# A filter, Mamba and FFN pipeline on one core: two convolution taps in one matmul, and the scan's products moved in TensorE's order

## The chip, the cores and the metric

The kernel runs on one core of one Trainium2 chip. A time is the device time of one execution in microseconds (us). The core has five engines that work at once and meet only through semaphores: TensorE (PE in the profile), VectorE (DVE), ScalarE (ACT), GpSimd (POOL) and SyncE (SP), whose queue issues the DMA transfers. Each engine takes its own instructions strictly in the order in which the program lists them.

## The reference

The input is 8 images of 64 channels and 128 x 128 pixels. Each goes through two layers.

Layer 0 is a filter with weights that depend on the pixel: a 3x3 convolution to 32 channels, a leaky ReLU, a 1x1 convolution to 9 values, and a softmax over them. With those weights `w_lp` the output is `x + sum over k of shifted_k(x) * (delta_k - w_lp_k)`. As `delta` picks the pixel itself, this is twice the pixel less the weighted mean of its nine neighbours.

Layer 1 takes that as `input` and does, cut to what matters:

```python
x_norm = ln4d(input, ...)                 # layer norm over the 64 channels
seq = layernorm(pixels as a sequence of 16384)
for i in range(2):
    seq = bimamba_block(seq, ...)         # forward and backward selective scan, 128 channels x 16 states
x4 = conv2d(rmsnorm(seq), resconv_w, pad=1)              # 3x3, 64 -> 64
x_mamba = x4 + res
dw = conv2d(conv2d(x_norm, dw1_w), dw2_w, groups=64, pad=1)   # 1x1, then depthwise 3x3
x = input + dw * x_mamba
g1, g2 = split(depthwise 3x3 of conv2d(ln4d(x), ffn_in_w))    # 64 -> 340
return x + conv2d(gelu(g1) * g2, ffn_out_w)
```

## The kernel before, in words

Four kinds of work are laid beside each other. The **scan** (class `Chunk`) is the main one: for each image, two layers by two directions by 16 chunks of 1024 pixels, 512 chunks in all. A chunk has U = 16 steps; a step is one scan instruction over 128 (channel, state) rows by 1024 pixels. An image has therefore 1024 steps, and the run 8192. Beside the scan of image b run three background jobs, each in 16 tiles of eight image rows (two halves of four rows stand on the two halves of the partitions):

- **Front** (layer 0 and the norms) of image b + 1, from step 569 of the image on, one tile each 24 steps;
- **Mix** (the two 3x3 convolutions, the product with `dw`, a norm) of image b, around the change to the next image, one tile each 13 steps;
- **FFN** of image b, beside steps 180 to 560 of the next image, one tile each 24 steps.

The front of image 0 runs ahead of the first scan, and partly beside it. The FFN of image 7 runs alone at the end, while its mix stands beside the end of its own scan.

Order is written out by hand. Each piece of work is put down with `at(time, phase, function)`. A step has the phases FEED, SCAN, MID, PROD, DECAY and REST, in this order. At the end the pieces are taken by (step, phase), and within one such place in the order in which they were put down; chunks put theirs down before front, mix and FFN do. Every engine's instruction list follows from that, and so does SP's queue of transfers.

One step of the scan works like this. `drive` (L1048) lets POOL multiply `bu` from `dup` and `bp` for two steps at a time, into three buffers. `decay` (L1053) lets ACT write exp(dt * A) to `w`, in one of two PSUM buffers. `scan` (L1063) is DVE's. `product` (L1092) multiplies by C, on DVE or, for some steps, on POOL. `collect` (L1103) sums over states in TensorE, into the single bank `y`. So that these have their inputs, each chunk needs main products in TensorE two chunks ahead: `conv` (L922, tile xp), `gate` (L938, zp), `step` (L967, dp) and `bc` (L984, bcp), and behind the second direction `project` (L1142, op), means (ms) and spread (rb). All of these share one PSUM bank, "mm": each product waits until ACT (or DVE) has read the one before. They are put in the phase FEED, and their evictions by ACT in DECAY of the same step or the next (L1177 on).

Background uses two further banks, "acc" and "bg". In the front, `hidden` (L450) is the first 3x3 convolution, nine matmuls of one tap each over a window `xa` with the two halves' weights as diagonal blocks; `weight` (L505) spreads the nine softmax weights over channels, `weighted` (L515) multiplies with the window `xb` on DVE, and `gather` (L519) sums the nine products in TensorE, onto a first matmul with `ident2`, twice the identity, that puts in the doubled pixel. In the mix, `conv` (L653) does the depthwise and the full 3x3 convolution in the same way, nine matmuls each of 128 x 128. The FFN's `conv` (L740) already takes two taps a matmul: the window is loaded twice, the second copy shifted by one pixel, on the two halves of the partitions. `rest_times` (L818) is DVE's product of the gelu's last 42 channels.

Tiles of 512 pixels in SBUF come from one ring, `tmp` (L402, 14 buffers), windows from another, `win` (L405, 2 buffers).

Of the kernel before, what the change touches and what calls it, by code (L numbers as in the profile page):

```python
# [15 lines left out]
P = 128  # L16
C = 64
# [38 lines left out]
def kernel(ctx: ExitStack, tc: tile.TileContext, a: dict, out: bass.AP):  # L56
# [15 lines left out]
    def const(shape, name, dt=F32):  # L72
        return wp.tile(shape, dt, tag=name, name=name)
# [47 lines left out]
    nc.vector.memset(half_mean[C:P, 1:2], 1.0 / C)  # L121
    ident2 = const([P, P], "ident2")
    nc.vector.tensor_tensor(ident2, ident, ident, ALU.add)

    sel_k = const([54, 9, 2, C], "sel_k", BF16)
    for h in range(2):
        k18 = [
            identb[0:54, 18 * i + 9 * h : 18 * i + 9 * h + 9]
            .rearrange("k (m o) -> k m o", o=1).to_broadcast([54, 9, C])
            for i in range(3)  # L130
        ]
        nc.vector.tensor_tensor(sel_k[:, :, h, :], k18[0], k18[1], ALU.add)
        nc.vector.tensor_tensor(sel_k[:, :, h, :], sel_k[:, :, h, :], k18[2], ALU.add)
    nc.vector.tensor_scalar(sel_k, sel_k, -1.0, None, ALU.mult)


# [28 lines left out]

    FRONT_W, MIX_W, FFN_W = 9 * 64 + P, 18 * P, 18 * P + 2 * C + P + 2 * 9
    w_dram = [dram([P, n], f"w{i}") for i, n in enumerate((FRONT_W, MIX_W, FFN_W))]

    def front_weights(t):
        return t[:, 0 : 9 * 64].rearrange("p (k m) -> p k m", m=64), t[:, 9 * 64 : FRONT_W]  # L170

    def mix_weights(t):
        v = t[:, 0:MIX_W].rearrange("p (i k m) -> p i k m", i=2, m=P)
        return v[:, 0], v[:, 1]

# [5 lines left out]
    with tc.tile_pool(name="wspill", bufs=1) as fp, tc.tile_pool(name="wprep", bufs=2) as pp, \  # L181
            tc.tile_pool(name="wps", bufs=4, space=PSUM) as pps:
        wt = [fp.tile([P, n], F32, tag=f"w{i}", name=f"w{i}") for i, n in enumerate((FRONT_W, MIX_W, FFN_W))]
        w1, dw1 = front_weights(wt[0])
        dw2, wres = mix_weights(wt[1])
        wpair, wlast, wout_a, wout_b, win_b, wtap_b = ffn_weights(wt[2])

# [18 lines left out]
        def diagonal(col, n):  # L206
            d = pp.tile([P, P], F32, tag="diag", name="diag")
            nc.vector.tensor_scalar(d[0:n, 0:n], ident[0:n, 0:n], col, None, ALU.mult)
            return d[0:n, 0:n]

        for t in wt:
            nc.gpsimd.memset(t, 0.0)
# [14 lines left out]
        for k in range(9):  # L227
            to_blocks(w1[:, k, :], turned(w1t[:, k, :], ident[0:32, 0:32], P, 32), C, 32)
            to_blocks(wres[:, k, :], turned(resv[:, k, :], ident[0:C, 0:C], P, C), C, C)
            nc.vector.tensor_scalar(dw2[:, k, :], ident, dw2n[:, k : k + 1], None, ALU.mult)  # L230
        w2n = pp.tile([9, 32], F32, tag="w2n", name="w2n")
# [153 lines left out]
    def tmp(name):  # L385
        return wk.tile([P, N], F32, tag="tmp", name=name, bufs=14)

    def window(img, name):

        return inp.tile([P, ROWS + 2, PW], F32, tag="win", name=name)  # L390

# [7 lines left out]
    def tap(win, k):  # L399
        i, j = divmod(k, 3)  # L400
        return win[:, i : i + ROWS, j : j + W]
# [38 lines left out]
    class Front:  # L440
# [4 lines left out]

        def load_x(self, name):
            setattr(self, name, window(x_img, name))
            load_window(getattr(self, name), x_img, self.c)

        def hidden(self, i):  # L450
            w1, _ = front_weights(Bg.weights)
            if i == 0:
                self.hp = acc_tile("hp")
            for k in range(3 * i, 3 * i + 3):
                nc.tensor.matmul(self.hp[0:64, :], w1[:, k, :], tap(self.xa, k), start=(k == 0), stop=(k == 8))

# [44 lines left out]
        def turned(self):  # L501
            self.wt = wk.tile([54, N], BF16, tag="wt", name="wt", bufs=2)
            nc.scalar.copy(self.wt, self.tp.rearrange("p r w -> p (r w)"))

# [14 lines left out]
        def gather(self, k):  # L519
            if k == 0:  # L520
                self.acc = acc_tile("acc")
                nc.tensor.matmul(self.acc, ident2, tap(self.xb, 4), start=True, stop=False)
            nc.tensor.matmul(self.acc, ident, self.t.pop(k), start=False, stop=(k == 8))  # L523

# [23 lines left out]
        def pointwise(self):  # L548
            _, dw1 = front_weights(Bg.weights)
            self.dp = acc_tile("dwp")  # L550
            nc.tensor.matmul(self.dp, dw1, self.xn, start=True, stop=True)
# [29 lines left out]
        def plan(self, a):  # L581
            n1, n2, n3 = self.n1, self.n2, self.n3
            b = a - FRONT_STEP
            self.alone = a + FRONT_STEP < -2
            at(b - 5, REST, self.load_x, "xa")
            for i in range(3):
# [12 lines left out]
            at(b + 32, DECAY, self.turned)  # L599
            at(a + 6, REST, self.load_x, "xb")  # L600
            for k in range(9):
# [46 lines left out]
    class Mix(Front):  # L648
        def load_conv(self, img, name):
            setattr(self, name, window(img, name))  # L650
            load_window(getattr(self, name), img, self.c)

        def conv(self, which, win, i):  # L653
            w = mix_weights(Bg.weights)[which]
            if i == 0:
                self.cv = acc_tile("cv")
            for k in range(3 * i, 3 * i + 3):
                nc.tensor.matmul(  # L658
                    self.cv, w[:, k, :], tap(getattr(self, win), k), start=(k == 0), stop=(k == 8 and which == 0)
                )  # L660

# [27 lines left out]
        def plan(self, a):  # L689
            n1 = self.n1  # L690
            at(a - 5, REST, self.load_conv, dw_img[self.p], "dww")
            at(a - 4, REST, self.load_conv, xm_img, "xmw")
            at(a - 1, REST, self.load_h)
            for i in range(3):
                at(a + i, REST, self.conv, 0, "dww", i)
                at(a + 3 + i, REST, self.conv, 1, "xmw", i)
            at(a + 3, DECAY, self.branch_out)
            at(a + 2, REST, self.load_x1)
            at(a + 5, REST, self.add_h)
            at(a + 8, DECAY, self.times)  # L700
            at(a + 8, REST, self.plus)
            at(a + 10, REST, self.store_x2)
            at(a + 10, REST, self.centered, bg_tile, "x1")
            at(a + 11, DECAY, self.centered_out)
            at(a + 12, REST, lambda: n1.means(bg_tile, self.sq))
            at(a + 13, DECAY, n1.means_out)
            at(a + 13, REST, n1.root)
            at(a + 16, REST, n1.spread, bg_tile)
            at(a + 17, DECAY, self.scaled, n1)
            at(a + 17, DECAY, self.norm)  # L710
            at(a + 17, REST, self.store_rows, xn_img, "hc")
# [7 lines left out]
    class Ffn:  # L719
# [6 lines left out]
        def load(self, h):  # L726
            if not self.alone:
                self.win[h] = window(xn_img, "fw")
            else:
                if h == 0:  # L730
                    self.fw = wk.tile([P, 2, T], F32, tag="bu", name="fw", bufs=3)
                self.win[h] = self.fw[:, h, 0 : (ROWS + 2) * PW].rearrange("p (r w) -> p r w", w=PW)
            for i in range(2):
                lo = PW * first_row(self.c, h) + i
                nc.sync.dma_start(
                    self.win[h][C * i : C * i + C].rearrange("p r w -> p (r w)"),
                    xn_img[:, lo : lo + (ROWS + 2) * PW],
                )

# [113 lines left out]
        def plan(self, a):  # L853
# [19 lines left out]
            at(a + gelus, REST, self.gelus)  # L873
            at(a + gelus + 1, DECAY, self.rest_times)
            at(a + out - 5, REST, self.load_x2)
# [18 lines left out]
    class Chunk:  # L894
# [97 lines left out]
        def bc_out(self):  # L992
            self.bcs = wk.tile([64, N], F32, tag="bc", name="bc", bufs=1)
            nc.scalar.copy(self.bcs, self.bcp[0:64, :])

# [181 lines left out]
        def plan(self):  # L1177
            b = self.t0 - 2 * U
            at(b + 3, REST, self.load_hn)
            for h in range(2):  # L1180
                at(b + 7 + h, FEED, self.conv, h)
                at(b + 7 + h, DECAY, self.conv_out, h)
                if self.second:
                    at(b + 9 + h, FEED, self.gate, h)
                    at(b + 9 + h, DECAY, self.gate_out, h)
                at(b + 14 + h, FEED, self.step, h)
                at(b + 14 + h, DECAY, self.step_out, h)
# [4 lines left out]
            b = self.t0  # L1192
            at(b - 16, FEED, self.bc)
            at(b - 16, DECAY, self.bc_out)
# [34 lines left out]
            at(b + 2, REST, self.load_h)  # L1229
            at(b + 5, FEED, self.project)  # L1230
            at(b + 6, DECAY, self.residual)
            at(b + 6, DECAY, self.square)
            if self.l == 0:
                at(b + 7, REST, self.store_h)
            at(b + 12, FEED, lambda: n.means(mm_tile, self.sq))
            at(b + 13, DECAY, n.means_out)
            at(b + 14, REST, n.root)
            at(b + 17, FEED, n.spread, mm_tile)
            at(b + 18, DECAY, self.normed)
# [52 lines left out]
```

## Time and profile before

| what | value |
|---|---|
| median of 3 runs | 29687.24 us (29686.83 to 29689.91) |
| the profiled execution | 29750.91 us, its span 29749.1 us |
| first scan starts, last scan ends | at 581 us and 29290 us of the span |
| busy: DVE, POOL, PE, ACT | 92%, 93%, 81%, 62% of the span |
| mean granted TensorE clock | 0.88 of full speed |
| DMA traffic | 6617.94 MB, 222 GB/s |

A row of groups in the profile gives the line, the engine, the operation, the tiles (out<-in), the shape and the count; then the busy time of the group, the mean time of one, and the engine's idle time before them with what ended it. A row of waits gives engine, tile and line of what waited, what it waited for, the sum in us, how often, and the longest. In a stretch of the timeline, the idle time before an instruction stands in brackets.

### The profile page before, as it was taken

The page shows a single profiled execution, that of the slowest core. Times are in us where ns is not written, and L with a number is a line of the kernel's source. Part 1 is how long each engine was busy: PE and PEld are TensorE (multiplying, and loading weights), DVE is VectorE, ACT ScalarE, POOL GpSimd, SP SyncE. Part 2 cuts the span into 40 slices and gives each one's busy share as a digit, 9 for nine tenths or more (in the row PEclk, how much of TensorE's full clock was granted, in tenths as well). Part 3 has the DMA queues.
Part 4 walks back from the last instruction along what each step waited for, and adds up shares of the span by engine and source line. Part 5 has one row for each costly group of instructions (what it writes and reads, how often), then busy time and mean ns, then how long its engine had stood idle before and what let it go on. Part 6 is the DMA issues. An engine that isn't in the chain of part 4 may idle for free. (4 is left out here: it accounts for less than half of the span.)

```text
span 29749.1 us, 307276 instructions
## 1 busy us (share of the span) xinstructions
PE 24131.5 (81%) x95804; PEld 8066.2 (27%) x95804; DVE 27302.9 (92%) x17562; ACT 18550.1 (62%) x28366; POOL 27655.0 (93%) x8732
## 2 busy tenths in 40 slices
PE   7766888878888788887888788887888878888578
PEld 3211332223322233222332223222232222322123
DVE  3999999999999999999999999999999999999996
ACT  2666666666666666666666666666666666666663
POOL 2999999999999999999999999999999999999993
PEclk8777888988889888988889888998898988989789
DMA  4676677767777677776777767777676766777674
GB/s 99 219 246 218 218 233 233 238 212 222 237 232 235 211 227 236 236 231 211 231 233 237 227 213 233 234 237 222 217 233 229 242 219 220 234 231 240 212 238 124
DMA packets 2530818, 6617.94 MB, mean 222 GB/s; under 512 B 418982, under 2 KB 723382, under 8 KB 2526870
## 3 DMA queue, kind: packets, MB, share of 16 engines
q1 hardware_dynamic: 2529174, 6598.27, 69.4%
q8 instruction: 757, 12.40, 0.2%
q14 instruction: 887, 7.27, 0.1%
HBM read 5364.00 MB, written 1266.18 MB: 223 GB/s over the span
## 5 line engine op out<-in xcount | busy, mean ns | idle before, releaser
L1050 POOL TENSOR_TENSOR bu<-dup,bp 128x2048 f32<-128x2048 f32 x4096 | 18567.4, 4536 | 568.0 <-DVE w L1078 413.9
L1058 ACT ACTIVATE w<-dtp,a_neg 128x1024 f32<-128x1024 f32 x8192 | 9162.5, 1118 | 514.1 <-DVE hs L1076 318.6
L1100 DVE TENSOR_TENSOR hs<-w,cp 128x1024 f32<-128x1024 f32 x5360 | 6564.4, 1225 | 322.3 <-DMA cp<-bc_dram 90.2
L1097 POOL TENSOR_TENSOR hs<-hs,cp 128x1024 f32<-128x1024 f32 x2832 | 6677.2, 2358 | 180.4 <-ACT state L1090 116.2
L1076 DVE TENSOR_TENSOR_SCAN w<-w,state,bu 128x1024 f32<-128x1024 f32 x2677 | 6281.0, 2346 | 349.9 <-ACT w L1058 349.1
L1078 DVE TENSOR_TENSOR_SCAN w<-w,state,bu 128x1024 f32<-128x1024 f32 x2683 | 6290.8, 2345 | 312.5 <-ACT w L1058 311.9
L1116 PE MATMUL y<-hs,sel_y 128*32 128x512 f32 x32768 | 5185.5, 702 | 30.3 <-POOL hs L1097 30.0
L1090 ACT COPY state<-w 128x1 f32<-128x1 f32 x5360 | 836.7, 156 | 5064.1 <-DVE hs L1100 5028.9
L1076 DVE TENSOR_TENSOR_SCAN hs<-w,state,bu 128x1024 f32<-128x1024 f32 x1419 | 3321.0, 2340 | 55.4 <-PE y L1116 28.2
L1078 DVE TENSOR_TENSOR_SCAN hs<-w,state,bu 128x1024 f32<-128x1024 f32 x1413 | 3307.3, 2341 | 54.6 <-ACT w L1058 37.6
L1109 PE MATMUL y<-xc,dskip 128*64 128x512 f32 x4096 | 1635.9, 867 | 2009.1 <-ACT yv L1133 1334.8
L928 PE MATMUL xp<-hn,wx 128*128 128x512 f32 x4096 | 2262.7, 680 | 447.8 <-ACT xc L934 344.2
L760 PE MATMUL fp<-fw,bgw 128*128 128x512 f32 (+1 forms) x5760 | 2276.1, 642 | 66.1 <-ACT ga L807 64.7
L1116 PEld LDWEIGHTS y<-hs,sel_y 128*32 128x32 f32 x32768 | 739.0, 117 | 3492.7 <-issue 2462.8
L1090 ACT COPY state<-hs 128x1 f32<-128x1 f32 x2832 | 540.6, 191 | 1827.8 <-DVE hs L1078 929.3
L421 POOL TENSOR_TENSOR r<-r,neg_half 128x8 f32<-128x8 f32 x768 | 1261.8, 1643 | 373.9 <-ACT r L418 312.3
L934 ACT ACTIVATE xc<-xp,cbias 128x512 f32<-128x512 f32 x1024 | 696.5, 680 | 1351.3 <-PE xp L928 1351.1
L969 PE MATMUL dp<-xc,wdt 128*128 128x512 f32 x2048 | 1214.9, 677 | 362.2 <-ACT dt L976 282.0
L1058 ACT ACT_TABLE_LOAD x1134 | 1454.9, 1283 | 20.1
L766 PE MATMUL fp<-fw,bgw 64*128 64x512 f32 (+1 forms) x5760 | 1415.6, 610 | 0.0
L1006 POOL TENSOR_TENSOR dt<-dt,xc 128x1024 f32<-128x1024 f32 x512 | 1211.0, 2365 | 207.9 <-DMA dt_dram<-dt 186.4
L523 PE MATMUL acc<-t,ident 128*128 128x512 f32 x2304 | 1369.5, 679 | 4.3 <-DVE t L517 4.3
(198 smaller groups left out, 27172.3 us busy)
## 6 DMA issues: line engine op xcount, KB each, us to landing
bp<-bc_dram SPq DMA_DIRECT2D x4096, 256.0 KB, 4.1
dup<-du_dram SPq DMA_DIRECT2D x4096, 256.0 KB, 5.0
dtp<-dt_dram SPq DMA_DIRECT2D x4096, 256.0 KB, 5.0
cp<-bc_dram SPq DMA_DIRECT2D x4096, 256.0 KB, 5.0
hn<-hn_dram SPq DMA_DIRECT2D x1024, 256.5 KB, 5.0
dt_dram<-dt SPq DMA_DIRECT2D x512, 512.0 KB, 3.4
du_dram<-dt SPq DMA_DIRECT2D x512, 512.0 KB, 2.6
yf_dram<-yv SPq DMA_DIRECT2D x512, 256.0 KB, 4.5
```

The costliest lines, as they stand in the source:

```text
L760: nc.tensor.matmul(o, wpair[:, i, g, m], self.win[h][:, i : i + ROWS, 0:W], start=(i == 0), stop=False)
L766: nc.tensor.matmul(o, wlast[rows, i, g, m], self.win[h][rows, i : i + ROWS, lo : W + lo], start=False, stop=(i == 2),)
L928: nc.tensor.matmul(self.xp[h], wx[:, self.l, self.d, i, :], self.hn2[:, s.start + 2 * i : s.stop + 2 * i], start=(i == 0), stop=(i == 1),)
L1050: nc.gpsimd.tensor_tensor(bu, self.dup[self.pairs[k][1]], self.over_pair("bp", k), ALU.mult)
L1058: nc.scalar.activation(w, self.dtp[gp][:, i, :], AF.Exp, scale=a_neg[:, self.l, self.d, g, j : j + 1])
L1076: nc.vector.tensor_tensor_scan(to, w, bu, s0, ALU.mult, ALU.add)
L1078: nc.vector.tensor_tensor_scan(to[:, ::-1], w[:, ::-1], bu[:, ::-1], s0, ALU.mult, ALU.add)
L1090: nc.scalar.copy(self.column(u), h[:, T - 1 : T] if self.d == 0 else h[:, 0:1])
L1097: nc.gpsimd.tensor_tensor(hs, hs, c, ALU.mult)
L1100: nc.vector.tensor_tensor(hs, w, c, ALU.mult)
L1109: nc.tensor.matmul(self.y[C * h : C * h + C, :], dskip[:, self.l, self.d, C * gp : C * gp + C], self.xc[:, s], start=True, stop=False,)
L1116: nc.tensor.matmul(self.y[lo : lo + 32, :], sel_y, hs[:, i, s], start=False, stop=(k % 4 == 3))
```

## The change

Five things are changed together.

1. The hidden convolution of the front and both convolutions of the mix use `two_halves`, which does for them what the FFN's convolution did: a window of each half is loaded twice, shifted by one pixel; the taps j = 0 and 1 of a row are one matmul of 128 rows, and the tap j = 2 is a matmul over the 64 rows of the half. For nine taps there are 12 matmuls, each for one half's columns, in place of 9 for both.
2. `ident2` and its matmul go. The bias row of ones is added to the transposed softmax weights `wt` (row 64, so 65 rows in place of 54), and the selector `sel_k` has 2 there for tap 4: the weight of the middle tap comes out as 2 less its softmax weight.
3. The products conv, gate, step, bc, project, means and spread of a chunk that isn't beside a front move from FEED of step t to REST of step t - 1.
4. `rest_times` moves from DECAY of the step after the gelus to MID of the step behind that.
5. The ring `tmp` has 12 buffers in place of 14 and takes the tile bc too; `win` has 4 in place of 2.

```diff
-    sel_k = const([54, 9, 2, C], "sel_k", BF16)
+    sel_k = const([65, 9, 2, C], "sel_k", BF16)
+    nc.vector.memset(sel_k, 0.0)
+    nc.vector.memset(sel_k[64:65, 4], -2.0)
...
+    wts = [const([65, N], f"wt{i}", BF16) for i in range(2)]
+    for t in wts:
+        nc.vector.memset(t, 0.0)
+        nc.vector.memset(t[64:65, :], 1.0)
...
-    FRONT_W, MIX_W, FFN_W = 9 * 64 + P, 18 * P, 18 * P + 2 * C + P + 2 * 9
+    FRONT_W, MIX_W, FFN_W = 6 * 32 + P, 12 * C, 18 * P + 2 * C + P + 2 * 9
...
-        return wk.tile([P, N], F32, tag="tmp", name=name, bufs=14)
+        return wk.tile([P, N], F32, tag="tmp", name=name, bufs=12)
...
-        return inp.tile([P, ROWS + 2, PW], F32, tag="win", name=name)
+        return inp.tile([P, ROWS + 2, PW], F32, tag="win", name=name, bufs=4)
+
+    def load_shifted(dst, img, c, h):
+
+        for i in range(2):
+            lo = PW * first_row(c, h) + i
+            nc.sync.dma_start(
+                dst[C * i : C * i + C].rearrange("p r w -> p (r w)"), img[:, lo : lo + (ROWS + 2) * PW]
+            )
+
+    def two_halves(outs, pair, last, wins, part, start=True, stop=True):
+
+
+        for h, o in enumerate(outs):
+            nc.tensor.matmul(
+                o, pair[:, part, :], wins[h][:, part : part + ROWS, 0:W], start=start and part == 0, stop=False
+            )
+        for h, o in enumerate(outs):
+            rows, lo = slice(C * h, C * h + C), 2 - h
+            nc.tensor.matmul(
+                o, last[rows, part, :], wins[h][rows, part : part + ROWS, lo : W + lo],
+                start=False, stop=stop and part == 2,
+            )
...
-            for k in range(3 * i, 3 * i + 3):
-                nc.tensor.matmul(self.hp[0:64, :], w1[:, k, :], tap(self.xa, k), start=(k == 0), stop=(k == 8))
+            two_halves([self.hp[32 * h : 32 * h + 32, :] for h in range(2)], pair, last, self.xa, i)
...
-            self.wt = wk.tile([54, N], BF16, tag="wt", name="wt", bufs=2)
-            nc.scalar.copy(self.wt, self.tp.rearrange("p r w -> p (r w)"))
+            self.wt = wts[self.c % 2]
+            nc.scalar.copy(self.wt[0:54, :], self.tp.rearrange("p r w -> p (r w)"))
...
-                nc.tensor.matmul(self.acc, ident2, tap(self.xb, 4), start=True, stop=False)
-            nc.tensor.matmul(self.acc, ident, self.t.pop(k), start=False, stop=(k == 8))
+            nc.tensor.matmul(self.acc, ident, self.t.pop(k), start=(k == 0), stop=(k == 8))
...
-            for k in range(3 * i, 3 * i + 3):
-                nc.tensor.matmul(
-                    self.cv, w[:, k, :], tap(getattr(self, win), k), start=(k == 0), stop=(k == 8 and which == 0)
-                )
+            outs = [self.cv[C * h : C * h + C, :] for h in range(2)]
+            two_halves(outs, pair, last, getattr(self, win), i, stop=(which == 0))
...
-            at(a - 5, REST, self.load_conv, dw_img[self.p], "dww")
-            at(a - 4, REST, self.load_conv, xm_img, "xmw")
+            for h in range(2):
+                at(a - 6 + h, REST, self.load_conv, dw_img[self.p], "dww", h)
+                at(a - 4 + h, REST, self.load_conv, xm_img, "xmw", h)
...
-            at(a + gelus + 1, DECAY, self.rest_times)
+            at(a + gelus + 2, MID, self.rest_times)
...
-            self.bcs = wk.tile([64, N], F32, tag="bc", name="bc", bufs=1)
+            self.bcs = tmp("bc")
...
+            def feed(t, fn, *args):
+                if self.beside_front:
+                    at(t, FEED, fn, *args)
+                else:
+                    at(t - 1, REST, fn, *args)
+
...
-                at(b + 7 + h, FEED, self.conv, h)
+                feed(b + 7 + h, self.conv, h)
                 at(b + 7 + h, DECAY, self.conv_out, h)
...
-                at(b + 14 + h, FEED, self.step, h)
+                feed(b + 14 + h, self.step, h)
...
-            at(b - 16, FEED, self.bc)
+            feed(b - 16, self.bc)
...
-            at(b + 5, FEED, self.project)
+            feed(b + 5, self.project)
```

Gate, means and spread change in the same way as conv.

## The prediction

> **What bounds the kernel now.** I read the page's first part, then three stretches of the fourth image: mix beside the scan, FFN beside it, front beside it. They are bounded by scan starts; each image has 1024 scan steps.
>
> ```profile
> PE 24131.5 (81%) x95804; PEld 8066.2 (27%) x95804; DVE 27302.9 (92%) x17562; ACT 18550.1 (62%) x28366; POOL 27655.0 (93%) x8732
> ...
> 11370.60:12026.90 656.30, 544.13 (x2043) 191.53 (x2043) 615.04 (x354) 409.36 (x615) 640.40 (x199) 0.89 0.74 234
> 12026.90:13294.70 1267.80, 1081.91 (x4319) 328.88 (x4314) 1194.58 (x713) 836.10 (x1227) 1195.12 (x347) 0.92 0.72 234
> 13294.70:14978.50 1683.80, 1369.94 (x5661) 476.72 (x5661) 1565.69 (x1063) 1071.25 (x1696) 1628.14 (x549) 0.87 0.70 222
> ```
>
> (Columns: stretch, length, busy time of PE, weight load, DVE, ACT, POOL, clock, DMA share, GB/s.) DVE and POOL are nearly level and nearly full. So a matmul saved is worth nothing by itself; it counts only where it shortens idle time of DVE, and POOL allows no more than its own idle: 15.9 us in mix, 72.7 in FFN, 55.7 in front. What ends DVE's and POOL's idle time, from the waits of the FFN stretch:
>
> ```profile
> DVE gt L819 <- ACT gt L814: 25.9, 16, 2.2
> DVE w L1078 <- ACT w L1058: 23.5, 14, 2.4
> DVE w L1076 <- ACT w L1058: 5.1, 5, 1.3
> DVE hs L1078 <- ACT w L1058: 4.7, 5, 1.1
> ...
> POOL bu L1050 <- DVE w L1078: 55.3, 31, 2.6
> POOL bu L1050 <- DVE w L1076: 9.0, 6, 2.9
> ...
> ACT xc L934 <- PE xp L928: 76.6, 31, 4.7
> ACT dt L976 <- PE dp L969: 46.4, 23, 4.2
> ACT bc L994 <- PE bcp L987: 21.5, 10, 2.8
> ```
>
> Here DVE leads: POOL's waits (64.3 us) are for a `bu` buffer that DVE's scan frees. DVE waits 25.9 us for the gelu and 33.3 us for the decay `w` that ACT makes. Why ACT is late is seen at 12.0 ms, PE's timeline, then ACT's:
>
> ```profile
> 12002.19 1.07 PE L1116 MATMUL y<-hs,sel_y 128*32 128x512 f32 x8
> 12003.19 1.99 PE L766 MATMUL fp<-fw,bgw 64*128 64x512 f32 x8
> 12005.11 1.99 PE L928 MATMUL xp<-hn,wx 128*128 128x512 f32 x4
> ...
> 12007.13 0.69 ACT L934 ACTIVATE xc<-xp,cbias 128x512 f32<-128x512 f32 x1 [2.38 <-PE xp L928]
> ```
>
> The scan's own product xp stands behind 1.9 us of FFN convolution. ACT, in order, waits 2.38 us to evict it, and the next decay is that much later. In the mix stretch DVE's waits are 21.3 us for `w` and 10.8 us for the background's norm product (hc L542 from rb); in front 38.8 us for `w` and 40.8 us for rb.
>
> **1. Main products first.** Outside the front, conv, gate, step, bc, project, means and spread move from the first phase of step t (FEED) to the last of t-1 (REST), registered before every background product of that step: PE runs them ahead of one step of background. At the example xp could start when ACT has freed the single mm bank (12003.2, the end of the previous xc) instead of 12005.1, so the 2.38 us wait shrinks by 1.9. Over the whole run 233 of the 236 us that DVE waits for `w` beside the FFN come within 9 us of an ACT wait for PE; I take three quarters away: 33.3 x 0.75 = 25 us an image. The added cost: PE now blocks on ACT's eviction of the bank with the background queued behind it. Six of 16 steps have such a hand-over (second conv, both gates, second step, bc, spread). FFN results have two steps of slack (times at 19 after conv at 17), so I cost this at 0 there, covered by PE's idle 185.9 us of 1267.8. Mix results have one step: branch_out, centered, means, spread, four a tile; 16 tiles x 4 x 6/16 = 24 a mix at 0 to 1.9 us (the FFN group above, waited out the other way), 0 to 46 us an image; I take 6, near the low end, because part 3 shortens PE's work there.
>
> **2. Gelu product a step later.** rest_times goes from DECAY of step gelu+1 to MID of gelu+2, behind one more scan (2.35 us). The idle before it is 25.9/16 = 1.6 us, less than that scan, so the wait is gone: -25.9, with 2 left for the odd ones. Behind it now: DVE's product of that step, 0.69 us later, and the bg bank, wanted again by conv at step 14, still a step off: 0. If that cover failed PE would wait up to 0.69+2.35 us, 16 times an image.
>
> FFN sum: DVE -24 -25 = -49 us. POOL allows less: in the mix stretch it is idle 15.9/656.3 = 2.4%, and at that share its 1195.1 busy us need 1224.7, a gain of 43. I take 40; x7 images = **-280**. In mix 21.3 x 0.75 = 16 less 6, but POOL has only 5.7 us that wait for DVE: -3 x7 = **-20**.
>
> **3. Convolutions with two taps a matmul.** Per convolution of 9 taps: 9 full matmuls become 6 of 128 rows (two column halves) and 6 of 64 rows (two quadrants). Every f32 matmul is two records here. Rows of the same forms, from the groups kept apart by form:
>
> ```profile
> L658 PE MATMUL cv<-dww,bgw 128*128 128x512 f32 x2304 | 1143.3, 641 | 3.8 <-DMA bgw<-w_dram 3.8
> L455 PE MATMUL hp<-xa,bgw 128*64 128x512 f32 x2304 | 1064.7, 608 | 66.4 <-DMA bgw<-w_dram 53.0 <-DMA xa<-x_dram 8.3 <-DMA dup<-du_dram 5.1
> L760 PE MATMUL fp<-fw,bgw 128*64 128x512 f32 x2688 | 640.2, 612 | 64.7 <-ACT ga L807 64.7
> L766 PE MATMUL fp<-fw,bgw 64*64 64x512 f32 x2688 | 626.1, 597 | 0.0
> L522 PE MATMUL acc<-xb,ident 128*128 128x512 f32 x256 | 157.9, 702 | 87.1 <-DVE hc L542 86.9
> ```
>
> Before: 18 x 0.496 = 8.9 us. After: 12 x 0.238 + 12 x 0.233 = 5.65, and four or five more changes of shape. Two rules of the Trainium skill speak against it (TensorEngine Tiling (Array Packing)). One, in Tiling Modes, Key Properties, says a change of tiling mode drains TensorE. It gives no price. In the PE timeline above, fp's 8 records take 1.92 us to the next start against 4 x 0.43, xp's 4 take 1.91 against 1.72: about 0.2 us a change, so +0.6 a convolution after the changes that it had anyway. The other, in Restrictions and Gotchas (PSUM pressure), says that different row tiles cannot access one PSUM bank at once. The two quadrants of a tile do just that, in bank cv. By the rule their 12 records would go one by one, 12 x 0.43 = 5.2, and the convolution would cost 2.86 + 5.2 + 0.6 = 8.6, no gain. But the fp row of 64*64 has this form (both halves into one bank) and costs 0.233 a record, half of 0.43: here they overlap. I take the row: 8.9 - 6.25 = 2.7 us a mix convolution, hidden conv 8.3 - 6.25 = 2.05 (its 32-column form has no row; between 0.158 of y's four at a time and 0.43). PE: 256 x 2.7 + 128 x 2.05 = 950 us.
>
> **4. Doubled pixel in the weight.** The row L522 goes: 1.2 us x 128 = 158 us of PE. The weight product grows from 54 to 65 rows: same 512 columns, 0.
>
> PE is not the bound, so parts 3 and 4 give: beside the front 16 x (2.05 + 1.2) = 52 us of PE's 1370, 4%, less lateness; of DVE's 79 us of waits for `w` and rb I take 10%: -8. Before the scan begins it is different: from 180 to 581 us PE is busy 340 of 401 us, so the nine or so tiles there gain 3.25 x 9 = 29, and the smaller weight image some more: **-33**. The last image's mix, where of 72.8 us of DVE idle in the last 440 steps 16 are waits for `w` behind PE and 33 for rb: a fifth, **-10**.
>
> **5. Loads and buffers.** xa, dww, xmw are loaded twice (shifted copy): 4 issues for 2, 400 KB more, 384 times = 154 MB on 6618. In mix 0.8 MB per 45 us, 18 GB/s on 234; its DMA share would be near 0.8. DVE's DMA waits there are none, in front 11.7 us: +2 an image. Behind each window on SP's queue stand the loads of bp, dup, dtp, cp; SP waits 2937 us for POOL at one of them, so the issues fit. The tmp ring falls from 14 to 12 and now also takes bc. In the programs' order the shortest reuse beside the front falls from five steps to two (28 times yv after a t that PE reads) and three (161 times), which is about PE's lateness there: 0 to 1.6 us (the mean of an rb wait) x 189 = 0 to 300; I take 28 x 0.5 = 14, as PE works within a step otherwise. Front: -8 x7 + 14 + 14 = **-28**.
>
> **Sum:** -280 -20 -28 -33 -10 = -371 on the span of 29749.1 (its execution took 29750.9) = 29378. The median shown is 63.7 us under that execution; the same 371 gives 29316. A little for new waits that I cannot place (a tenth): **29,350**.
>
> **The rivals.**
> (a) *POOL takes over at once* (0.18). For: its 96% beside mix and front. Then DVE's saved waits return as waits for bu, and half of the FFN gain remains: -140 -33 -10, 29,505. Against: its idle beside FFN is 64.3 us of waits for DVE alone.
> (b) *Nothing is gained in the scan* (0.05): DVE's waits were ACT's own lateness through two w banks; only the part before the scan remains, 29,655, within 0.2%.
> (c) *PE blocks with the background behind it* (0.15), slower. Place: the six hand-overs in each 16 steps beside mix and FFN. If each costs PE 1.5 us idle, that is 9 us of a 55 us stretch, where PE has 8.1 idle (185.9/1267.8): PE becomes the bound, and rb and fp come late to DVE. At 2% of 1924 us x 7 it costs 270, against 71 that the rest still gives: 29,886. It decides from about 1.3 us a hand-over. Against: convolutions are shorter beside mix, and ACT has (1267.8 - 836.1)/368 = 1.2 us a step to spare.
>
> **How the numbers follow.** Main case 0.62, (a) 0.18, (b) 0.05, (c) 0.15. Main and (a) are faster: 0.80; (b) 0.05; (c) 0.15. 0.2%, about 60 us, is what a measurement of this kernel can tell from no change. Main case alone: 29,210 (all of POOL's 64.3 us in six or seven FFNs) to 29,470. The 8 in 10 range takes in (a): 29,190 to 29,620.
>
> **What would show it.** Beside FFN: DVE's wait gt from gt near zero, w from ACT at a third or less, POOL idle under 40 us an image, and the stretch near 1228. ACT's waits for xp, dp, bcp less than half. cv rows at 128*64 and 64*64 near 0.24 us a record. The prediction is wrong if the cv rows of 64*64 cost 0.43, if PE's idle for ACT (xc, gate, bc) beside FFN grows past 186 us, or if hc from rb grows in mix.

## The result, and the profile after

The changed kernel takes 29468.39 us (median of 4 runs, 29464.12 to 29487.03) against 29687.04: a ratio of 0.9929 (95% interval 0.9915 to 0.9944), 219 us less. The forecast was 29,350, 337 less. The direction and the range hold; about two thirds of the forecast gain came, and it came largely from other places than forecast.

The first part of the page after, then the same three stretches of the fourth image (length; busy time of PE, weight load, DVE, ACT, POOL; clock, DMA share, GB/s):

```profile
PE 23428.5 (80%) x97852; PEld 7363.8 (25%) x97852; DVE 27280.7 (93%) x17559; ACT 18566.1 (63%) x28357; POOL 27653.4 (94%) x8732
...
11268.80:11914.00 645.20, 495.97 (x2198) 133.42 (x2198) 614.17 (x353) 412.05 (x617) 637.40 (x199) 0.88 0.79 252
11914.00:13177.10 1263.10, 1087.27 (x4316) 326.74 (x4312) 1193.39 (x713) 834.99 (x1223) 1197.15 (x347) 0.91 0.71 235
13177.10:14846.00 1668.90, 1317.59 (x5762) 446.31 (x5762) 1564.52 (x1064) 1071.93 (x1699) 1629.01 (x550) 0.85 0.71 229
```

DVE's and POOL's work is unchanged, as it should be. Mix is 11 us shorter, front 15, and the FFN stretch only 4.7, where 40 were forecast. Its waits after:

```profile
DVE w L1117 <- ACT w L1097: 20.3, 22, 1.2
DVE hs L1117 <- issue: 17.5, 11, 1.8
...
DVE ga L861 <- PE fp L805: 4.1, 5, 0.9
...
DVE hs L1117 <- ACT w L1097: 1.4, 1, 1.4
...
DVE w L1115 <- ACT w L1097: 1.2, 1, 1.2
...
ACT w L1097 <- DVE hs L1117: 37.7, 22, 2.1
ACT xc L973 <- PE xp L967: 31.1, 16, 3.6
ACT dt L1015 <- PE dp L1008: 25.9, 19, 3.0
```

and one row of the waits of the same stretch before:

```profile
ACT w L1058 <- DVE hs L1078: 3.7, 5, 0.8
```

The wait for gt (25.9 us) is gone. In its place stands one that was not there, 17.5 us before a scan, put down to nothing that the profile shows ("issue"). ACT waits for xp only 31.1 us, where it was 76.6, so the main products do come earlier. But DVE's wait for `w` fell from 33.3 only to 22.9 (20.3, 1.4 and 1.2), and ACT now waits 37.7 us for a scan of DVE's before it may write `w`; that row was 3.7 us before. These two new waits are what the experiments are about.

Over the whole run, by scan starts, the profiled executions differ as follows (us; beside the FFN split by the direction that the scan runs, since only the second direction has gates and the norm). The profiled execution before lay 64 us above its median, so the spans differ by 287 us and not 219 (3 us the other way lie in the first 192 steps of image 0, which are not listed). The FFN's rows, here and below, take in the same steps of image 0, where no FFN runs; 11 of the 27 us lie there. Forecast were -33 before the first scan, -20 beside mix, -280 beside the FFN, -28 beside the front, -10 in the last steps and nothing for the FFN alone.

| stretch | before | after | difference |
|---|---|---|---|
| before the first scan | 581 | 539 | -42 |
| beside mix (7 times) | 4615 | 4539 | -75 |
| FFN, first direction | 3011 | 2945 | -66 |
| FFN, second direction | 7054 | 7081 | +27 |
| beside front (7 times) | 11861 | 11783 | -78 |
| last 440 scan steps | 1483 | 1440 | -43 |
| FFN alone at the end | 459 | 447 | -12 |

### The profile page after: what moved, and what is told of

It is laid out like the page before. It is cut to its first block, busy times and chain, and to the rows that moved or that the text cites. A ratio compares the mean times of both kernels' runs of the same rounds, so it can differ in the third digit from the quotient of the medians.

```text
span 29462.3 us, 312607 instructions
## 1 busy us (share of the span) xinstructions
PE 23428.5 (80%) x97852; PEld 7363.8 (25%) x97852; DVE 27280.7 (93%) x17559; ACT 18566.1 (63%) x28357; POOL 27653.4 (94%) x8732
## 5 line engine op out<-in xcount | busy, mean ns | idle before, releaser
L1117 DVE TENSOR_TENSOR_SCAN w<-w,state,bu 128x1024 f32<-128x1024 f32 x2683 | 6290.5, 2345 | 302.1 <-ACT w L1097 301.0
L1117 DVE TENSOR_TENSOR_SCAN hs<-w,state,bu 128x1024 f32<-128x1024 f32 x1413 | 3308.4, 2341 | 183.3 <-issue 121.2
L1115 DVE TENSOR_TENSOR_SCAN hs<-w,state,bu 128x1024 f32<-128x1024 f32 x1419 | 3321.2, 2340 | 38.6 <-PE y L1155 17.5
L1148 PE MATMUL y<-xc,dskip 128*64 128x512 f32 x4096 | 1571.0, 856 | 1656.3 <-ACT yv L1172 1383.9
L967 PE MATMUL xp<-hn,wx 128*128 128x512 f32 x4096 | 2353.8, 704 | 653.6 <-ACT xc L973 476.2
L967 PEld LDWEIGHTS xp<-hn,wx 128*128 128x128 f32 x4096 | 830.6, 216 | 1967.7 <-issue 961.4
```

The lines of the kernel that those rows point to most:

```text
L967: nc.tensor.matmul(self.xp[h], wx[:, self.l, self.d, i, :], self.hn2[:, s.start + 2 * i : s.stop + 2 * i], start=(i == 0), stop=(i == 1),)
L1115: nc.vector.tensor_tensor_scan(to, w, bu, s0, ALU.mult, ALU.add)
L1117: nc.vector.tensor_tensor_scan(to[:, ::-1], w[:, ::-1], bu[:, ::-1], s0, ALU.mult, ALU.add)
L1148: nc.tensor.matmul(self.y[C * h : C * h + C, :], dskip[:, self.l, self.d, C * gp : C * gp + C], self.xc[:, s], start=True, stop=False,)
```

## The experiments

Ratios are to runs of the kernel before on the same chip, whose median there was 29739 to 29773 us.

### One part at a time

**Main products first, alone** (on the kernel before).

```diff
-                at(b + 7 + h, FEED, self.conv, h)
+                feed(b + 7 + h, self.conv, h)
...
```

> Part 1 alone on the kernel before: conv, gate, step, bc, project, means and spread go ahead of one step of background, outside the front; convolutions, buffers and the gelu product stay. My theory, from the trace after: main products first helps where the scan runs a first direction and costs where it runs a second one (gates, project, norm in the same bank). Expected: 40 to 110 us less than before; of the FFN's stretches the ones beside first-direction chunks some 60 us shorter over the run, the ones beside second-direction chunks longer by 0 to 60. Rival: the moves of order are worth nothing by themselves and all of the gain comes from shorter convolutions; then within 30 us of before.

Measured: 29686.9 us, 0.9972 (0.9961 to 0.9983), 86 us less. FFN stretches: -64 beside the first direction, -28 beside the second; DVE's waits for `w` there fell from 236 to 107 us. The order helps by itself; the loss beside the second direction that I expected from gates and norm did not come, so it has another cause. Beside mix it did not help (+40 us over the run). DVE's waits in the mix stretch of the fourth image, before and in this run:

```profile
DVE w L1076 <- ACT w L1058: 21.3, 19, 1.9
DVE hc L542 <- PE rb L427: 10.8, 4, 3.6
```

```profile
DVE hc L542 <- PE rb L427: 25.8, 10, 5.0
DVE w L1076 <- ACT w L1058: 12.6, 12, 1.2
```

The wait for `w` falls there too, and the one for the background's rb grows by more; over the run, hc from rb beside mix goes from 85 to 200 us.

**The gelu product, alone** (on the kernel before).

```diff
-            at(a + gelus + 1, DECAY, self.rest_times)
+            at(a + gelus + 2, MID, self.rest_times)
```

> Part 2 alone on the kernel before: DVE's product of the gelu's last channels one scan later. My theory: ACT is what is late after the gelus (two table loads and three gelus before the next decay), so DVE's wait of 174 us for gt moves to the scan of the step three behind the gelu and at most a third of it is gained: 0 to 60 us less than before. Rival, the prediction's step: the wait is hidden behind the scan, about 170 us less.

Measured: 29739.1 us, 0.9988 (0.9980 to 0.9997), 34 us less. Beside the FFN DVE's wait for gt went from 174 us to 0, and the wait before a scan ("issue") from 0 to 128. The wait moved. Mix, which this run leaves as it was, is 29 us longer in its profiled execution than before: a difference of a stretch of some 30 us between two single executions says little.

**Convolutions, loads and buffers, alone** (the changed kernel with the old places of the main products and of the gelu product).

```diff
-            at(a + gelus + 2, MID, self.rest_times)
+            at(a + gelus + 1, DECAY, self.rest_times)
...
             def feed(t, fn, *args):
-                if self.beside_front:
-                    at(t, FEED, fn, *args)
-                else:
-                    at(t - 1, REST, fn, *args)
+                at(t, FEED, fn, *args)
```

> Parts 3 to 5 alone: convolutions of two taps a matmul with their doubled loads, the pixel in the weight, 12 buffers in the ring, with the old places of the main products and of the gelu product. My theory: the head 40 us shorter, the last image's mix and the tail some 40 us, mix and front beside the scan together 60 to 120 us: 120 to 200 us less than before, the larger part of the whole. Rival, the prediction's sizes: about 70 us less.

Measured: 29569.3 us, 0.9933 (0.9918 to 0.9947), 204 us less: mix -74, front -107, start -26, last steps -23, end -11. So this part alone is worth as much as all of the change. But beside the FFN, whose code it doesn't touch, it lost 57 us (60 in the second direction, less 3 in the first).

**The gelu product back**, in the changed kernel.

> The changed kernel with the gelu product back in DECAY of the step after the gelus. My theory (the wait only moves): within 40 us of the changed kernel, DVE waiting again some 170 us for gt and none for the scan behind it. Rival: 120 us or more slower than the changed kernel.

Measured: 29532.3 us, 0.9920 (0.9905 to 0.9934), against 0.9929 with the move: no difference to be seen. DVE waited 147 us for gt again.

### Where the gelu's wait went

The changed kernel at one FFN tile, ACT's timeline, then DVE's:

```profile
5074.32 0.69 ACT L1015 ACTIVATE dt<-dp,dtb 128x512 f32<-128x512 f32 x1 [2.10 <-PE dp L1008]
5075.03 1.28 ACT L853 ACT_TABLE_LOAD   x1
5076.32 0.60 ACT L853 ACTIVATE gt<-fp 128x512 f32<-128x512 f32 x1
5076.81 1.14 ACT L855 ACTIVATE ga<-ga 128x512 f32<-128x512 f32 x2
5077.85 0.15 ACT L1129 COPY state<-w 128x1 f32<-128x1 f32 x1
5078.02 1.28 ACT L1097 ACT_TABLE_LOAD   x1
5079.32 1.12 ACT L1097 ACTIVATE w<-dtp,a_neg 128x1024 f32<-128x1024 f32 x1
...
5077.56 1.22 DVE L1139 TENSOR_TENSOR hs<-w,cp 128x1024 f32<-128x1024 f32 x1
5080.52 2.35 DVE L1117 TENSOR_TENSOR_SCAN hs<-w,state,bu 128x1024 f32<-128x1024 f32 x1 [1.75 <-issue]
```

From 5075.03 to 5079.32 ACT makes no decay: two table loads and three gelus. The scan that starts at 5080.52 needs the decay that ends at 5080.44. DVE hardly stands at gt any more, and stands before that scan instead, for 1.75 us. To see whether the detour is the cause, exp takes gelu's place beside the scan, which needs no table loads:

```diff
-                nc.scalar.activation(self.gt, self.rest[0], AF.Gelu)
+                nc.scalar.activation(self.gt, self.rest[0], AF.Exp)
             for h in range(2):
-                nc.scalar.activation(self.ga[h], self.ga[h], AF.Gelu)
+                nc.scalar.activation(self.ga[h], self.ga[h], AF.Gelu if self.alone else AF.Exp)
```

> The changed kernel with exp in place of gelu wherever the FFN stands beside a scan, so that ACT needs no table load before and after; the output is not the reference's. Theory (the wait of the gelu product came back because ACT's next decay stands behind three gelus and two table loads of 1.28 us): DVE's idle time of 121 us before the scan three steps behind the gelus goes, and the FFN's stretches are 100 to 250 us shorter over the run. Rival: something else holds that scan (its hs buffer, freed by TensorE): the idle time stays above 80 us.

Measured: 29273.9 us (one run). The idle time of 121 us is 0.2, and the FFN's stretches are 213 us shorter. What DVE waited for before the backward scans (L1117), over the run, in us and times:

```profile
  ACT w L1097: 300.3, 260
...
  issue: 0.2, 1
```

The three activations take as long as before (0.59 and 0.63 us each, where the gelus took 0.60 and 0.62), so the two table loads are what the scan waited for. That the wait for gt at the old place came from the same detour is not shown by a run of its own; it follows from the wait that moved. The waits for `w` stay at 300 us: they are another matter.

### The bank of the decay

In the convolutions' run one of a chunk's 16 steps grew most beside the FFN's second direction (40 us over the run, from the third scan of the chunk to the fourth), and nothing of the convolutions runs there. ACT's timeline at one such step in the kernel before, and then in the run with the buffers alone (below), which shows the same:

```profile
12580.27 0.58 ACT L994 COPY bc<-bcp 64x512 f32<-64x512 f32 x1 [2.12 <-PE bcp L987]
12580.75 0.15 ACT L1090 COPY state<-w 128x1 f32<-128x1 f32 x1
12580.94 1.12 ACT L1058 ACTIVATE w<-dtp,a_neg 128x1024 f32<-128x1024 f32 x1
```

```profile
12606.02 0.58 ACT L994 COPY bc<-bcp 64x512 f32<-64x512 f32 x1 [2.12 <-PE bcp L987]
12606.51 0.15 ACT L1090 COPY state<-w 128x1 f32<-128x1 f32 x1
12607.89 1.12 ACT L1058 ACTIVATE w<-dtp,a_neg 128x1024 f32<-128x1024 f32 x1 [1.23 <-DVE hs L1078]
...
12605.51 2.34 DVE L1078 TENSOR_TENSOR_SCAN hs<-w,state,bu 128x1024 f32<-128x1024 f32 x1
...
12609.04 2.36 DVE L1078 TENSOR_TENSOR_SCAN w<-w,state,bu 128x1024 f32<-128x1024 f32 x1 [0.47 <-ACT w L1058]
```

The same decay starts at once in the one, and waits 1.23 us in the other, for the scan that is running. The two programs say why. `w` has two PSUM buffers under one tag, and which of them a decay gets is settled when the program is built, not in turn. In most places decay u gets the buffer of decay u - 2. In some it gets that of decay u - 1, which is still to be scanned, though the other is free. Then ACT can't run ahead, and DVE waits for it. Such repeats are 384 of 8192 decays in the kernel before, 309 with main products first alone, 494 with the convolutions and buffers alone, 412 in the changed kernel. Beside the FFN's second direction they are 70, 70, 155 and 155, of the 155 each 15 in image 0. In the trace before, 527 of the 772 us that DVE was idle before scans stand at those 384 places; in the changed kernel 435 of 774 at its 412.

**Buffers alone**: the ring of 12, with bc in it, on the kernel before.

```diff
-        return wk.tile([P, N], F32, tag="tmp", name=name, bufs=14)
+        return wk.tile([P, N], F32, tag="tmp", name=name, bufs=12)
...
-            self.bcs = wk.tile([64, N], F32, tag="bc", name="bc", bufs=1)
+            self.bcs = tmp("bc")
```

> The buffers of part 5 alone on the kernel before: ring of 12, bc in it, windows as before. Its program has 494 repeated banks, as the run with the convolutions alone has, 85 more than before beside second-direction chunks with the FFN. Theory: 30 to 80 us slower than before, 60 of them in those stretches, and nothing beside mix and front. Rival (the prediction's part 5): waits for the ring beside the front, some 14 us there, and 0 elsewhere.

Measured: 29821.1 us, 1.0019 (1.0012 to 1.0026), 55 us slower; beside the FFN's second direction +59 (11 of them in image 0, where no FFN runs), beside front -2. Of what I expected, the place and the size hold; mix, where I had expected no difference, was 21 longer, which is within what two single executions differ by.

**Banks in turn**: a tag of its own for even and for odd steps. The tiles of the front and the FFN that share these banks before and after the scans take the two tags by turns.

```diff
-            w = pw.tile([P, T], F32, tag="w", name="w")
+            w = pw.tile([P, T], F32, tag=f"w{u % 2}", name="w", bufs=1)
```

> The changed kernel with the two PSUM banks of the decay w taken strictly in turn (a tag for even and one for odd steps), nothing else. In the program of the changed kernel 412 of 8192 decays are written to the same bank as the decay before them, so that ACT must wait for a scan that is still to come; in the trace 435 of DVE's 774 us of idle time before scans stand just there. Theory: that is a cost by itself; 150 to 350 us less than the changed kernel, beside the FFN with second-direction chunks most of it. Rival: where the banks repeat ACT was late anyway, the choice follows from that and costs nothing; within 50 us of the changed kernel.

> The kernel before with the two banks of w in turn: 384 repeats there, with 527 us of DVE's idle time before scans. Theory: 150 to 350 us less than before, and DVE's waits for w fall to under a half. Rival: within 50 us of before; what the changed kernel gains is then not tied to the banks.

Measured: the changed kernel with banks in turn 29230.7 us, 0.9820 (0.9804 to 0.9837); the kernel before with banks in turn 29604.6, 0.9946 (0.9932 to 0.9961). So repeats cost the changed kernel 1.1%, some 320 us, and the kernel before 0.5%, 162. Of the former 165 lie beside the FFN's second direction, 31 beside its first and 63 beside mix. For the kernel before the waits for `w` did not fall to under a half as I expected (beside the FFN 236 to 177): there ACT is still late because of TensorE (in the FFN stretch of the fourth image it waits 77.2 us for xp, 76.6 before). With main products first it is so much less (24.6 us in the changed kernel with banks in turn), and the banks are what is left. The FFN stretch of the fourth image and its waits, changed kernel with banks in turn:

```profile
11829.80:13065.00 1235.20, 1080.70 (x4316) 323.05 (x4312) 1191.84 (x714) 837.49 (x1224) 1195.71 (x347) 0.92 0.73 240
...
DVE hs L1117 <- issue: 9.3, 6, 2.1
...
DVE w L1117 <- ACT w L1097: 1.4, 3, 0.6
...
POOL bu L1089 <- DVE w L1117: 18.0, 13, 2.0
```

The wait for `w` is 1.4 us, and the stretch 32.6 us shorter than before the change; 40 was forecast.

**The parts with banks in turn.** Two runs more take the change apart on this ground: the convolutions and buffers alone, and all but the move of the gelu product. Their edits are those above, with the two tags.

> Parts 3 to 5 alone (as in the run of the convolutions alone), with the banks of w in turn. Beside before with banks in turn (0.9946 of before) it shows what the convolutions and buffers are worth when the bank choice is out of play. Theory: head, mix, front, last mix and tail as in the run of the convolutions alone, and the loss of 57 us beside the FFN gone: 0.987 to 0.990 of before. Rival: the loss beside the FFN comes from the ring or the doubled loads themselves and stays: 0.991 or more.

> The changed kernel with banks of w in turn (0.982 of before) and the gelu product back at its old place. Theory: with decays no longer held up, ACT comes out of the gelus with one decay in hand, and the move of the product is worth something now: 30 to 110 us slower than with the move, 0.983 to 0.986. Rival: the wait only moves, as it did before: within 25 us.

Measured: 0.9885 (0.9870 to 0.9900) and 0.9831 (0.9816 to 0.9845). The loss of 57 us beside the FFN is gone (-11 against the kernel before with banks in turn). In steps, from 0.9946: convolutions and the rest -0.6%, main products first -0.5%, gelu product -0.1%, the last within the intervals.

| step, us | as built | banks in turn |
|---|---|---|
| convolutions, pixel, buffers | -199 | -181 |
| main products first | -39 | -161 |
| gelu product | +27 | -33 |
| all | -211 | -375 |

(Each from its ratio and 29,750; a ratio's interval is some 40 us to either side, so the gelu product's sign is open in both columns.) Main products first gained 160 us beside the FFN with banks in turn: from the convolutions' run to the run without the gelu move, both with banks in turn, DVE's waits for `w` there went from 175 to 19 us.

**Main products first beside the front as well.**

```diff
             def feed(t, fn, *args):
-                if self.beside_front:
-                    at(t, FEED, fn, *args)
-                else:
-                    at(t - 1, REST, fn, *args)
+                at(t - 1, REST, fn, *args)
```

> The gelu product at its old place, main products ahead of the background also beside the front, banks of w in turn; to be set against the run with the gelu product at its old place alone. Theory: beside the front DVE waits more for norm products of the background (262 us there for rb) than it gains in waits for w (219 us): 20 to 150 us slower. Rival: as beside mix, DVE's waits for w fall to a third and it is 50 to 150 us faster.

The expectation names the gelu product's place wrongly: this kernel has it at the new place, so it is to be set against 0.9820. Measured: 0.9908 (0.9891 to 0.9925), about 260 us slower, 191 of them in the front stretches. DVE's waits in the front stretch of the fourth image, with the exception beside the front and then without it:

```profile
DVE hn L617 <- PE rb L467: 19.3, 8, 4.3
DVE w L1117 <- ACT w L1097: 17.1, 10, 3.2
...
DVE w L1115 <- ACT w L1097: 14.5, 11, 3.3
DVE hc L585 <- PE rb L467: 6.5, 5, 2.2
```

```profile
DVE t L561 <- PE wb L557: 41.9, 19, 7.2
DVE hn L617 <- PE rb L467: 29.5, 15, 3.4
DVE hc L585 <- PE rb L467: 16.6, 12, 2.7
...
DVE w L1117 <- ACT w L1097: 3.7, 6, 0.8
```

The waits for `w` go, and those for the front's own products (wb, rb) take their place and more. Over the run, t from wb beside the front goes from 14 to 290 us; DVE wants wb one step after it is queued.

## Why the prediction was right or wrong, point by point

**What bounds it.** DVE and POOL, and a saved matmul counts only through DVE's waits: this held. PE's busy time fell by 703 us and the span by far less. Rival (a), that POOL takes over, depends on the stretch. Beside the FFN it did not come: POOL still waited for DVE (28.1 us for `bu` in the fourth image), and was idle 66 us there, 39.5 with banks in turn, where under 40 was forecast. Beside mix it nearly did. The mix stretch above has POOL busy 637.4 of 645.2 us, and with banks in turn:

```profile
11190.50:11829.80 639.30, 504.45 (x2201) 134.89 (x2202) 613.46 (x354) 412.44 (x615) 637.64 (x199) 0.87 0.81 255
```

Over the seven mixes POOL is then idle 9 us of 4476, so what DVE still waits for there can't be turned into time without less work on POOL.

**Step 1, main products first: its mechanism was right, its size was not.** ACT's waits for TensorE fell as said, to less than half for xp and bcp (21.5 to 7.5), not quite for dp (46.4 to 25.9). The term that was mis-sized is "33.3 x 0.75 = 25 us an image": 10.4 came. I had put DVE's wait for `w` down to ACT's being late behind TensorE alone, because nearly all of those waits come shortly after such a one. The second cause was in the same places: the decay's bank. It can't be seen from the waits by themselves, only from a decay that waits for a scan while the other bank is free. Over the run the waits for `w` beside the FFN fell from 236 to 107 us with this step alone, but only to 171 in the changed kernel, whose smaller ring adds 70 repeats there. With banks in turn the step's size was, if anything, short: 33.3 to 1.4.

Two costs of step 1 were off. Beside the FFN I had 0 for late background results; DVE's wait for the convolution's tile fp (the row of ga) went from 0 to some 30 us over the run. Beside mix I had 6 us an image for late rb (rival c, in small): the step alone costs 16 (85 to 200 us over seven images), and 5 to 10 once the convolutions are shorter (29 to 67 us with banks in turn, 20 to 87 without). In the whole change hc from rb went only from 85 to 93 us, since the convolutions alone bring it down to 20. The sign that I had named, that it grows in mix, is thus true of the step and hidden in the sum. Beside the front, where the change doesn't make the move, rival (c) is what the last run shows.

**Step 2, the gelu product: failed.** The sentence "the wait is gone ... behind it now ... 0" looked at gt and not at what ACT does next. ACT was the one that was late; the scan three steps behind the gelus asked for the late decay, and DVE waited 121 us there where it had waited 174 for gt. What the move is worth, some 30 us at most, can't be told from nothing in the changed kernel.

**Step 3, convolutions.** The quadrants in one bank do overlap, as the row promised and against the rule cited. The rows after:

```profile
L422 PE MATMUL cv<-dww,bgw 128*64 128x512 f32 x1536 | 462.3, 683 | 0.0
L427 PE MATMUL cv<-dww,bgw 64*64 64x512 f32 x1536 | 440.4, 651 | 0.0
L422 PE MATMUL hp<-xa,bgw 128*32 128x512 f32 x1536 | 426.2, 621 | 46.3 <-DMA bgw<-w_dram 36.9 <-DMA xa<-x_dram 6.2 <-DMA dup<-du_dram 3.1
L427 PE MATMUL hp<-xa,bgw 64*32 64x512 f32 x1536 | 410.7, 611 | 0.0
```

In these rows a record is 0.28 to 0.30 us of busy time beside mix, not 0.235, and 0.27 to 0.28 in the 32-column form. But busy time counts the end of every short group as well. PE's timeline shows one third of a convolution of `dww`, from its start to the next product's:

```profile
11347.50 1.08 PE L422 MATMUL cv<-dww,bgw 128*64 128x512 f32 x4
11348.51 1.08 PE L427 MATMUL cv<-dww,bgw 64*64 64x512 f32 x4
11349.52 0.64 PE L1155 MATMUL y<-hs,sel_y 128*32 128x512 f32 x4
```

The four records over 64 rows take 1.01 us, where one by one they would take 1.72. The third takes 2.02 us, which is also the median of all that stand alone, so a convolution takes 6.05 us, and 6.25 was forecast. Counted in the same way, a third before took 2.68 to 2.77 us, so 8.0 to 8.3 us a convolution and not the 8.9 that I took from busy time: the gain is 2.0 to 2.3 us and not 2.7. A change of shape is cheaper than I estimated: two pairs of records start 0.47 us apart within one shape and 0.52 across a change, so some 0.05 us, not 0.2. What the convolutions were worth to the run, though, I put far too low: mix -74 and front -107 us alone, where the forecast gave the convolutions nothing of their own in mix and "10%" of the waits, 8 us an image, beside the front. TensorE's lateness, not its busy time, was what DVE met there: with banks in turn DVE's wait for hc from rb fell by two thirds beside both (89 to 29 us, 107 to 35), though hn from rb rose beside the front (161 to 195). The 10% was a guess and should have been called one.

**Step 4** needs no change: wb with 65 rows takes 0.432 us a record, 0.423 before. **The start** gave 42 us in the two executions compared, but that is a lucky pair: over all runs it lasts 573 to 581 us with the old code and 539 to 556 with the new, in the mean 25 less (33 said). The last steps gave 43 (10 said): 23 with the convolutions alone, the rest with the main products. The FFN alone gave 12, of which I had nothing.

**Step 5, buffers: failed in kind.** I costed the smaller ring at waits for a free buffer, 14 us beside the front. There were none to see (-2). But changing the ring gave 85 more decays a repeated bank in the second-direction steps, and cost 59 us where nothing of it runs. With banks in turn that loss is gone, so it was the banks and not the ring. The doubled loads brought mix's DMA share to 0.79, as forecast (near 0.8). DVE waits 6 us more for `cp` there over the run, and 25 to 42 us in the four runs of the changed convolutions with banks in turn, against 2 in the kernel before with banks in turn; POOL is idle only 9 to 13 us beside mix in those four, so these waits are not what sets the stretch.

**The sum.** With banks in turn the change is worth 375 us; 371 was the sum of the steps. The agreement is partly luck, since steps 2 and 3 were off in opposite directions: against the kernel before with banks in turn the FFN stretches gave 202 us where 280 were forecast, mix 71 where 20 were, and the last steps 42 where 10 were. What it lacked for the kernel as built is the bank: 375 - 211 = 164 us.

Why the build settles on a repeated bank in some places and not in others was not looked into; that the choice follows edits elsewhere, and what it costs, is shown.

## What to carry to other kernels

Where a two-buffer tile is what lets one engine run ahead of another, give its buffers by turns with a tag each, and look in the program, after every edit of buffers or order, whether they still alternate: here the two tags were worth more than the move of the main products as built. Before a waiting instruction is moved out of the way, ask what the engine that it waited for has to deliver next; if that engine is the late one, the wait comes back one instruction on. Moving main work ahead of background is a trade: it paid beside the FFN, whose results have two steps of slack, came out about even beside mix with one, and lost beside the front, where DVE takes nine wb a tile, each with one. That the slack decides is inferred from these three, not tested by itself.

## What the runs showed that I had not expected

A decay that waits for a scan with the other bank free: 1.23 us in the one shown, and 1.1% of the run for the 412 together, some 0.8 us each. And the gelu's detour of ACT: its two table loads are 1.28 us each, with the next activation right behind them, and without them the changed kernel's FFN stretches were 213 us shorter (one run). The fastest version that computes the reference is the changed kernel with banks in turn, 29230.7 us, 0.9820 of the kernel before.
